# The first norm of a transformer block: single loads, VectorE normalization, grouped transposes, and a query part moved behind the first scores

## The chip, the cores and the metric

The kernel runs on one NeuronCore of a Trainium2 chip. The core's engines each have an instruction queue of their own that runs in order: TensorE (PE; its weight loads are listed apart as PEld), VectorE (DVE), ScalarE (ACT), GpSimd (POOL) and SyncE (SP, which here only issues DMA transfers). The metric is the device time of one execution in microseconds. Three runs of the kernel before gave 1083.71, 1084.04 and 1085.92 us; the median is 1084.04 us.

## What is computed

One block over x of shape (2, 1024, 256): a self-attention with 16 heads of 64, a cross-attention to a context of shape (2, 154, 192), and a gated feed-forward. All numbers are 32-bit floats. Only the beginning matters here:

```python
h = _layernorm(x, ln1_g, ln1_b)        # (x - mean) * rsqrt(var + eps) * g + b, over the 256 features
q, k, v = h @ sa_wq, h @ sa_wk, h @ sa_wv
attn = softmax(q @ k.T * 64 ** -0.5)   # per head
x = (attn @ v) @ sa_wo + sa_bo + x
```

## The kernel before

The rows of one batch are 8 tiles of 128 rows. A tile is taken with the one 4 places on: the order is 0, 4, 1, 5, 2, 6, 3, 7, so that a pair (i, 4+i) fills both halves of the partitions after its transposition.

**The first norm** (`norm_pieces`, with `first` set) has four pieces. `stats` (L239, L240) finds mean and variance of a tile on DVE. `deviation` (L245, L249) takes a pair: DVE adds eps, POOL raises to the power -0.5. `normalize` takes a pair: DVE makes an offset (L255), then ACT normalizes one tile (L269) and POOL the other (L266). `turn` transposes a pair on PE, 4 transposes into two PSUM banks (L279); its `store` then applies gain and shift while it copies to `hT`, half of it on DVE (L290), half on ACT (L294). Gain and shift are columns loaded by four small transfers (L109).

**The first unit.** A unit is one batch and one pair of heads; there are 16. Its queries and keys are projections of `hT`. For the very first unit, `part(what, i)` projects the columns of pair i (16 matmuls of 128 columns, L361) and `take` copies a finished bank to `q_sa` or `k_sa`. The kernel projects queries and keys of pairs 0 and 1, keys of pairs 2 and 3, and the rest of the queries later.

**The self-attention steps.** Steps p = 0 to 127, eight for each unit, are written out by hand. `self_first(p)` issues on PE the scores of the step in two banks (32 matmuls, L492; called s0, s1, ... below), and on DVE a maximum for each bank (L501). `then()` issues on ACT the exponentials (L507), which free the two score banks one after the other. SP exchanges the maxima and sums between partitions by four small transfers `st<-st` (L517); from the next step on POOL (L525, L526, L612), ACT (`ee`, L532) and DVE (L604, and the block transposes L639) finish the weights of earlier steps. There are only two score banks, so the second half of s(p+1) waits for the last exponential of step p.

Between the scores of two steps PE does other work. `run_work` takes it from a list, `work`, in order, one piece that needs two PSUM banks per step: the rest of the queries (`self_queries`), the values of the first unit in two pieces (`value_pieces`, L392), then the queries, the keys and the values of the next unit. The two banks (`mm`) are shared by all these pieces: a piece may start when ACT has copied the result of the one before. One piece of a second list, `side`, goes with it: the context transposes (`pc`, L201), context keys (`pk`, L776), `p_rows` (L192). From p = 7 on the step's other work is the weighted values `po` (L546).

Copies of finished pieces stand in `stores` and are issued by `flush(stores)`, in the next step ahead of the exponentials.

**SP's order.** SP issues `x`, the small columns, `sa_wq`, `sa_wk`, `sa_wv` (L133) and so on. Transfers take eight completion semaphores in turn, so the ninth transfer on SP and ACT together is issued only when the first has landed. At step 0 the keys' weights of the second unit are loaded behind the exchange of step 0, and at step 1 its queries' weights behind the exchange of step 1.

In the compiled program PE's order from the first scores on is: s0, rest of the queries, pc, s1, values (first half), pk, s2, values (second half), pk x2, s3, queries of unit 1, p_rows, s4, keys of unit 1, s5, values of unit 1, s6, pk x2, s7, pk, po.

Of the kernel before, what the change touches and what calls it, by code (L numbers as in the profile page):

```python
# [18 lines left out]
def tile_transformer_block(ctx: ExitStack, tc: tile.TileContext, a: dict, out: bass.AP):  # L19
# [59 lines left out]
        for b in range(B) for g in range(NG)  # L79
    }  # L80

    def load_x(queue, b, t):

        queue.dma_start(
            out=xt[b, t // GT][:, t % GT:t % GT + 2, :],
            in_=x[b, t * P:(t + 2) * P, :].rearrange("(t p) d -> p t d", p=P),
        )


# [11 lines left out]
            n_cols = r + k  # L101
        r += k
    rows = pp_.tile([n_rows - n_cols, P], F32, tag="P", name="rows")
    for t in range(0, NT // 2, 2):
        load_x(nc.sync, 0, t)
        load_x(nc.scalar, 0, NT // 2 + t)
    for n in names[:2]:
        for r0 in range(0, P, HR):
            (nc.scalar if n == names[0] else nc.sync).dma_start(  # L109
# [110 lines left out]
    def norm_pieces(kind, b, first=False):  # L220
# [30 lines left out]

        def normalize(t):
            rstd = st["rstd", t]
            off = small.tile([P, 2], F32, tag="off", name=f"off_{ln}_{b}_{t}")
            nc.vector.scalar_tensor_tensor(  # L255
                off, st["mv", t][:, :, 0], -1.0, rstd, op0=ALU.mult, op1=ALU.mult
            )
            pool, tag = (one, "xn") if narrow(kind, b) and not first else (pp_, "P")

            xn = pool.tile([P, nh, 2, D // nh], F32, tag=tag, name=f"xn_{ln}_{b}_{t}")  # L260
            st["xn", t] = xn
            for i in range(2):
                xs = xt[b, order[t + i] // GT][:, order[t + i] % GT, :]
                xs, own = xs.rearrange("p (c d) -> p c d", c=nh), xn[:, :, i, :]
                if not narrow(kind, b) or first and i == 1:
                    nc.gpsimd.tensor_scalar(  # L266
                        own, xs, rstd[:, i:i + 1], off[:, i:i + 1], op0=ALU.mult, op1=ALU.add)
                else:
                    nc.scalar.activation(  # L269
                        own, xs, AF.Identity, bias=off[:, i:i + 1], scale=rstd[:, i:i + 1])  # L270

        def turn(t):

            n = 2 if first else 1
            bank = mm_tile if first and t == 2 else spare["bank"]
            ph = [bank(f"ph_{ln}_{b}_{t}_{i}") for i in range(n)]
            for i in range(2 * D // P):

                nc.tensor.transpose(  # L279
                    ph[i * n * P // (2 * D)][:, i % (2 * D // P // n) * P:][:, :P],  # L280
                    st["xn", t].rearrange("p c i d -> p (c i d)")[:, i * P:(i + 1) * P], ident)

            def store():
                k = NC * 2 * P // nh
                for c in range(nh):
                    own = st["hT"][:, c, t // 2 * k:(t // 2 + 1) * k]
                    turned = ph[c * n // nh][:, c % (nh // n) * k:][:, :k]
                    gain, shift = cols[:, g0 + c:g0 + c + 1], cols[:, b0 + c:b0 + c + 1]
                    if spare["turned"] or first and c < nh // 2:
                        nc.vector.tensor_scalar(  # L290
                            own, turned, gain, shift, op0=ALU.mult, op1=ALU.add
                        )
                    else:
                        nc.scalar.activation(own, turned, AF.Identity, bias=shift, scale=gain)  # L294

            return store
# [12 lines left out]
    def narrow(kind, b):  # L309

        return kind == "sa" or kind == "ca" and b < B - 1
# [929 lines left out]
    with tc.manual_schedule():  # L1241
# [19 lines left out]
        def take(what, i):  # L1261
            at = banks[what] if i < 2 else banks["k2"]
            take_both(qk["sa", 0, 0]["qk".index(what)], at, scale if what == "q" else None,
                      i * P, 2 * P, shared=True)


        for _ in range(27):
            nc.tensor.transpose(own[0][:, 1, :P], ident, ident)
        emit(stats[0], stats[1], deviation[0])
        emit(stats[2], stats[3], normalize[0], deviation[1], stats[4], normalize[1])  # L1270
        copies = [turn[0](), turn[1]()]
        copies[0]()
        part("q", 0)
        part("k", 0)
        emit(stats[5], deviation[2])
        copies[1]()
        emit(stats[6], normalize[2], stats[7], deviation[3])
        copies = turn[2]()
        part("q", 1)
        emit(normalize[3])  # L1280
        copies()
        part("k", 1)
        copies = turn[3]()
        banks["k2"] = two_banks("first_k")
        part("k", 2)
        copies()
        take("q", 0)
        take("k", 0)
        part("k", 3)
# [7 lines left out]
        side.append((True, (), lambda: together(*(  # L1297
            lambda pr=pr: context_keys(pr, sum_tile) for pr in (1, 2)))))
        side.append((True, (), turn_rows))
        work.append(costing(2, lambda: self_queries(*units[0], P, 2 * P)))  # L1300
        work.extend(value_pieces(*units[0], 2, False))

        for p in range(SA):
# [5 lines left out]
            then = self_first(p)  # L1309
            flush(stores)  # L1310
            then()
            if adds:
                adds.pop(0)()
            flush(kept)
# [190 lines left out]
```

## Time and profile before

| | |
|---|---|
| median of three runs | 1084.04 us |
| profiled execution | 1085.11 us, span of its instructions 1083.3 us |
| PE busy | 1067.4 us, 99% of the span |
| DVE, ACT, POOL busy | 889.9, 646.9, 765.0 us |
| granted TensorE clock | 1.0 |

A row of the timeline gives the start in us from the beginning of the span, the duration, engine, line, operation, what is written and read, and how many instructions the row merges. In brackets stands how long the engine was idle before it, and what ended that. The view of waits sums such idle times: us in total, times, longest. Lines in these views are those of the kernel before.

### The profile page before, as it was taken

The numbers are of one execution on the slowest core, as the hardware profiler recorded it, in microseconds if no ns is written. First come the engines' busy times: TensorE is split into PE (matmuls) and PEld (weight loads), VectorE is DVE, ScalarE is ACT, GpSimd is POOL, SyncE is SP. The second block draws the span as 40 slices with busy tenths as digits, with TensorE's granted clock in tenths as the row PEclk, the third lists the DMA queues.
The fourth block names the chain that finished last, engine by engine and source line by source line (L and its number), as shares of the span: only waits on it lengthen the run. The fifth ranks groups of instructions, "written<-read, shape, count | busy, mean of one in ns | idle before, by whom it ended". The sixth has DMA issues, their size and how long they took to land.

```text
span 1083.3 us, 45246 instructions
## 1 busy us (share of the span) xinstructions
PE 1067.4 (99%) x18548; PEld 710.0 (66%) x18548; DVE 889.9 (82%) x1317; ACT 646.9 (60%) x2063; POOL 765.0 (71%) x1600
## 2 busy tenths in 40 slices
PE   8999999999999999999999999998999999999998
PEld 6556556566565565565675665575777767888998
DVE  5789999998998989999999989968877887655554
ACT  5666767677666666666776766666566554342221
POOL 2667777788777777777777777757665686388774
PEclk9999999999999999999999999999999999999999
DMA  3232111111111111211211201136855545000000
GB/s 94 64 90 62 44 43 44 37 38 43 33 43 24 43 43 33 48 42 29 48 41 26 53 14 37 24 96 139 202 134 138 126 115 131 17 6 15 20 11 30
DMA packets 105120, 62.84 MB, mean 58 GB/s; under 512 B 32266, under 2 KB 95506, under 8 KB 104914
## 3 DMA queue, kind: packets, MB, share of 16 engines
q1 hardware_dynamic: 103586, 59.29, 23.2%
q8 instruction: 146, 2.39, 0.9%
q10 hardware_dynamic: 1328, 0.66, 0.2%
q14 instruction: 60, 0.49, 0.1%
HBM read 30.01 MB, written 2.10 MB: 30 GB/s over the span
## 4 chain that ended last, share of the span: by engine, by line
PE 87%; DVE 3%; DMA 3%; POOL 3%; ACT 2%; SPq 1%; issue 1%; DVEq 0%; POOLq 0%; ACTq 0%
PE s L492 19%; PE po L546 19%; PE py_sa L466 5%; PE py_ca L466 5%; PE pv_sa L392 5%; PE pq_ca L361 4%; PE pq_sa L361 4%; PE pk_sa L361 4%; PE poc L938 4%; PE pb L1062 3%; PE pf L1186 3%; PE sc L855 3%; PE pa L1062 2%; PE pc L1062 2%; DMA st<-st 2%; PE pf L1225 1%
## 5 line engine op out<-in xcount | busy, mean ns | idle before, releaser
L612 POOL TENSOR_SCALAR p<-p,rd,ee 128x512 f32<-128x512 f32 x508 | 387.3, 773 | 99.1 <-DVE rd L604 97.3
L507 ACT ACTIVATE p<-s,st 128x512 f32<-128x512 f32 x512 | 345.8, 686 | 176.5 <-DVE st L501 170.5
L501 DVE TENSOR_REDUCE st<-s 128x2 f32<-128x1024 f32 x256 | 308.5, 1206 | 51.7 <-issue 20.1
L639 DVE STREAM_TRANSPOSE pT<-p 128x1024 f32<-128x1024 f32 x256 | 302.3, 1219 | 1.5 <-POOL p L612 1.5
L492 PE MATMUL s<-k_sa,q_sa 64*32 64x512 f32 x4096 | 255.4, 591 | 2.7 <-ACT p L507 2.1
L546 PE MATMUL po<-pT,v_sa 64*32 64x256 f32 x8192 | 238.6, 376 | 0.9 <-ACT p L873 0.9
L546 PEld LDWEIGHTS po<-pT,v_sa 64*32 64x32 f32 x8192 | 173.8, 106 | 74.9 <-issue 27.3
L492 PEld LDWEIGHTS s<-k_sa,q_sa 64*32 64x32 f32 x4096 | 81.6, 106 | 102.8 <-issue 53.5
L873 ACT ACTIVATE p<-sc,neg 128x154 f32<-128x154 f32 x256 | 96.5, 408 | 84.5 <-DVE rden L881 80.7
L884 POOL TENSOR_SCALAR p<-p,rden 128x154 f32<-128x154 f32 x256 | 97.3, 401 | 62.7 <-DVE rden L881 62.3
L507 ACT ACTIVATION_READ_ACCUMULATOR p<-s,st 128x1 f32 x512 | 103.2, 202 | 0.0
L525 POOL TENSOR_TENSOR dd<-st 128x8 f32<-128x8 f32 x128 | 25.8, 202 | 66.1 <-DMA st<-st 64.3
L392 PEld LDWEIGHTS pv_sa<-sa_wv,hT_ln 64*128 64x128 f32 x1024 | 58.6, 188 | 14.2 <-issue 10.9
L392 PE MATMUL pv_sa<-sa_wv,hT_ln 64*128 64x128 f32 x1024 | 61.8, 275 | 0.0
L860 DVE TENSOR_REDUCE neg<-sc 128x6 f32<-128x924 f32 (+1 forms) x48 | 48.0, 1001 | 14.5 <-PE sc L855 14.4
L466 PE MATMUL py_ca<-ca_wo,o_ca 128*128 128x256 f32 x256 | 59.9, 382 | 0.0
L466 PE MATMUL py_sa<-sa_wo,o_sa 128*128 128x256 f32 x256 | 59.5, 386 | 0.0
L466 PEld LDWEIGHTS py_sa<-sa_wo,o_sa 128*128 128x128 f32 x256 | 47.3, 190 | 17.8 <-issue 6.9
L361 PE MATMUL pq_ca<-hT_ln,ca_wq 64*128 64x512 f32 (+1 forms) x352 | 58.4, 590 | 0.5 <-DMA ca_wq<-in_L_xattn_ca_wq_dram 0.5
L873 ACT ACTIVATION_READ_ACCUMULATOR p<-sc,neg 128x1 f32 x256 | 57.2, 224 | 0.0
L361 PE MATMUL pq_sa<-hT_ln,sa_wq 64*32 64x512 f32 (+1 forms) x976 | 57.0, 586 | 0.0
L361 PE MATMUL pk_sa<-hT_ln,sa_wk 64*32 64x512 f32 x960 | 56.8, 590 | 0.0
(135 smaller groups left out, 1471.5 us busy)
## 6 DMA issues: line engine op xcount, KB each, us to landing
wf<-pT_ca SPq DMA_DIRECT2D x128, 128.0 KB, 2.4
v_sa<-v_sa SPq DMA_DIRECT2D x32, 256.0 KB, 3.8
st<-st SPq DMA_DIRECT2D x510, 1.0 KB, 1.9
sa_wq<-in_L_xattn_sa_wq_dram SPq DMA_DIRECT2D x32, 128.0 KB, 3.4
sa_wk<-in_L_xattn_sa_wk_dram SPq DMA_DIRECT2D x32, 128.0 KB, 3.6
sa_wv<-in_L_xattn_sa_wv_dram SPq DMA_DIRECT2D x32, 128.0 KB, 3.3
ca_wq<-in_L_xattn_ca_wq_dram SPq DMA_DIRECT2D x32, 128.0 KB, 4.4
wf<-in_L_xattn_ff_w_dram SPq DMA_DIRECT2D x12, 256.0 KB, 4.2
```

The lines of the kernel that those rows point to most:

```text
L361: nc.tensor.matmul(pq[r][f:f + m, at:at + n], lhsT=wt[own, c, f:f + m], rhs=h[own, c, t0:t0 + n], start=(c == 0), stop=(c == NH - 1), tile ...
L392: nc.tensor.matmul(pv[r][:, i * P:(i + 1) * P], lhsT=h[own, c, i * P:(i + 1) * P], rhs=wt[own, c, :], start=(c == 0), stop=(c == NH - 1), ...
L466: nc.tensor.matmul(py[:, e * D:(e + 1) * D], lhsT=o[:, i, (t + e) * P:(t + e + 1) * P], rhs=wo[kind, b, g][:, i, :], start=(i == 0), stop= ...
L492: nc.tensor.matmul(sc[a4 * KB:(a4 + 1) * KB, j, :], lhsT=q[r, c:c + KB], rhs=k[r, h * HB:(h + 1) * HB], start=True, stop=True, tile_positi ...
L501: nc.vector.tensor_reduce(st[:, 0, 0, i, :], sc, AX.X, ALU.max, negate=True)
L507: nc.scalar.activation(pr[:, j, :], sc[:, j, :], AF.Exp, bias=st[:, 0, 0, i, j:j + 1], accum_out=st[:, 0, 1, i, j:j + 1],)
L546: nc.tensor.matmul(po[a2][d:d + KB, :QH // 2], lhsT=v[r, t, e, d:d + KB], rhs=pT[r, d // DH * NK + n, :], start=(t == 0 and e == 0), stop= ...
L612: nc.gpsimd.tensor_scalar(pr[:, j, :], pr[:, j, :], v["rd"][:, c:c + 1], v["ee"][:, 0, c:c + 1], op0=ALU.mult, op1=ALU.mult,)
L639: nc.vector.transpose(halves[h][:, :, c:c + KB], slot[p]["members"][i].rearrange("p j (n k) -> p (j n) k", k=KB))
L873: nc.scalar.activation(pr_[:, j, i, :T], sc[:, j, i * T:(i + 1) * T], AF.Exp, bias=neg[:, j, i:i + 1], accum_out=den[:, j, i:i + 1],)
L884: nc.gpsimd.tensor_scalar(pr_[:, j, i, :T], pr_[:, j, i, :T], rden[:, j, i:i + 1], 1.0, op0=ALU.mult, op1=ALU.mult,)
L1062: nc.tensor.matmul(into[:, :BT], lhsT=lhs, rhs=wh[pair][i], start=first, stop=True, skip_group_check=True)
```

## The change

1. The first loads: each of SP and ACT loads one tile, one tile and two tiles, instead of two and two. That is six transfers instead of four ahead of the columns and the weights.
2. `normalize` of the first norm runs on DVE alone, two instructions per pair that subtract the mean and multiply by the reciprocal deviation. The offset, the ACT and the POOL instruction fall away.
3. The pieces are issued in another order. On DVE: statistics of tiles 0, 4, 1 and 2, the normalization of pair 0, statistics of 5 and 6, the copy of pair 0, statistics of 3 and 7, the normalization of pairs 1, 2 and 3, their copies. On PE: transposes of pair 0, keys 0, queries 0, transposes of pairs 1, 2 and 3 in a row, keys 1, 2 and 3. Pairs 2 and 3 take one bank each. The filling transposes ahead are 23 instead of 27.
4. Queries of pair 1 are no longer projected before the first scores. The later piece covers 384 columns per half instead of 256. It is issued in step 0 directly, behind the exponentials, with its copy flushed at once, and is no longer an entry of `work`; so step 0 also takes the first entry that is left.

In the compiled program PE's order from the first scores on becomes: s0, rest of the queries (384), values (first half), pc, s1, values (second half), pk, s2, queries of unit 1, pk x2, s3, keys of unit 1, p_rows, s4, values of unit 1, s5, s6, pk x2, s7, pk, po. From there on the order is the same. SP still loads the queries' weights of unit 1 behind the exchange of step 1; the moves of the value tiles (L408, L409) come one step earlier in its queue. ACT's first activation is now the copy of pair 0, and its table load waits for the four column transfers; before it waited for the first x.

```diff
-    def load_x(queue, b, t):
+    def load_x(queue, b, t, n):
         queue.dma_start(
-            out=xt[b, t // GT][:, t % GT:t % GT + 2, :],
-            in_=x[b, t * P:(t + 2) * P, :].rearrange("(t p) d -> p t d", p=P),
+            out=xt[b, t // GT][:, t % GT:t % GT + n, :],
+            in_=x[b, t * P:(t + n) * P, :].rearrange("(t p) d -> p t d", p=P),
         )
...
-    for t in range(0, NT // 2, 2):
-        load_x(nc.sync, 0, t)
-        load_x(nc.scalar, 0, NT // 2 + t)
+    for t, n in ((0, 1), (1, 1), (2, 2)):
+        load_x(nc.sync, 0, t, n)
+        load_x(nc.scalar, 0, NT // 2 + t, n)
...
         def normalize(t):
             rstd = st["rstd", t]
+            if first:
+                xn = st["xn", t] = pp_.tile(
+                    [P, nh, 2, D // nh], F32, tag="P", name=f"xn_{ln}_{b}_{t}")
+                for i in range(2):
+                    xs = xt[b, order[t + i] // GT][:, order[t + i] % GT, :]
+                    nc.vector.tensor_scalar(
+                        xn[:, :, i, :], xs.rearrange("p (c d) -> p c d", c=nh),
+                        st["mv", t][:, i, 0:1], rstd[:, i:i + 1],
+                        op0=ALU.subtract, op1=ALU.mult)
+                return
...
         def turn(t):
-            n = 2 if first else 1
+            n = 2 if first and t < GT else 1
...
         def take(what, i):
             at = banks[what] if i < 2 else banks["k2"]
             take_both(qk["sa", 0, 0]["qk".index(what)], at, scale if what == "q" else None,
-                      i * P, 2 * P, shared=True)
-        for _ in range(27):
+                      i * P, P if what == "q" else 2 * P, shared=True)
+        for _ in range(23):
             nc.tensor.transpose(own[0][:, 1, :P], ident, ident)
-        emit(stats[0], stats[1], deviation[0])
-        emit(stats[2], stats[3], normalize[0], deviation[1], stats[4], normalize[1])
-        copies = [turn[0](), turn[1]()]
+        emit(stats[0], stats[1], deviation[0], stats[2], stats[4], normalize[0])
+        emit(stats[3], stats[5], deviation[1])
+        copies = turn[0]()
+        copies()
+        part("k", 0)
+        part("q", 0)
+        emit(stats[6], deviation[2], stats[7], deviation[3])
+        emit(normalize[1], normalize[2], normalize[3])
+        copies = [turn[1](), turn[2]()]
         copies[0]()
-        part("q", 0)
-        part("k", 0)
-        emit(stats[5], deviation[2])
         copies[1]()
-        emit(stats[6], normalize[2], stats[7], deviation[3])
-        copies = turn[2]()
-        part("q", 1)
-        emit(normalize[3])
+        copies = turn[3]()
+        part("k", 1)
         copies()
-        part("k", 1)
-        copies = turn[3]()
         banks["k2"] = two_banks("first_k")
         part("k", 2)
-        copies()
         take("q", 0)
         take("k", 0)
         part("k", 3)
...
-        work.append(costing(2, lambda: self_queries(*units[0], P, 2 * P)))
         work.extend(value_pieces(*units[0], 2, False))
...
             then = self_first(p)
             flush(stores)
             then()
+            if p == 0:
+                run(lambda: self_queries(*units[0], P, P))
+                flush(stores)
```

More of the change, by code (lines that the diff above doesn't have):

```diff
@@ L257, in normalize @@
             )
-            pool, tag = (one, "xn") if narrow(kind, b) and not first else (pp_, "P")
+            pool, tag = (one, "xn") if narrow(kind, b) else (pp_, "P")
             xn = pool.tile([P, nh, 2, D // nh], F32, tag=tag, name=f"xn_{ln}_{b}_{t}")
@@ L264, in normalize @@
                 xs, own = xs.rearrange("p (c d) -> p c d", c=nh), xn[:, :, i, :]
-                if not narrow(kind, b) or first and i == 1:
+                if not narrow(kind, b):
                     nc.gpsimd.tensor_scalar(
```

## The prediction

> **What bounds the kernel now.** I read the page's busy times first, then the waits of PE over the whole span, then PE's timeline through the first steps, and last the other queues at the places where PE's next piece would have to wait.
>
> ```profile
> PE 1067.4 (99%) x18548; PEld 710.0 (66%) x18548; DVE 889.9 (82%) x1317; ACT 646.9 (60%) x2063; POOL 765.0 (71%) x1600
> ```
>
> ```profile
> PE s L492 <- ACT p L507: 2.1, 5, 1.1
> PE ph_ln L279 <- POOL xn_ln L266: 2.0, 5, 0.9
> PE first L1268 <- POOL ident masks.py:199: 1.9, 1, 1.9
> ...
> PE s L492 <- DVE k_sa L382: 0.6, 1, 0.6
> ```
>
> PE is busy for 99% of the span, so only its idle time, or work taken from it, can be won, and any new idle time is lost. The second fence is PE's longest waits over the whole span. Most of the 2.0 and all of the 0.6 lie ahead of the first scores; they are what an earlier first norm can take away. The longest of the 2.1, 1.1, is the first place where the softmax, not PE, sets the pace.
>
> ```profile
> 9.48 1.16 PE L361 MATMUL first<-hT_ln,sa_wq 64*128 64x128 f32 x16
> 10.48 1.06 PE L361 MATMUL first<-hT_ln,sa_wk 64*128 64x128 f32 x16
> ...
> 14.24 0.66 PE L279 MATMUL ph_ln<-ident,xn_ln 128*128 128x128 f32 x4
> 14.82 2.06 PE L361 MATMUL first_k<-hT_ln,sa_wk 64*128 64x128 f32 x32
> 17.52 1.95 PE L492 MATMUL s<-k_sa,q_sa 64*32 64x512 f32 x32 [0.64 <-DVE k_sa L382]
> 19.40 2.00 PE L361 MATMUL pq_sa<-hT_ln,sa_wq 64*128 64x256 f32 x16
> 21.33 0.74 PE L201 MATMUL pc<-ident,cn 77*96 77x77 f32 x8
> 22.00 1.96 PE L492 MATMUL s<-k_sa,q_sa 64*32 64x512 f32 x32
> 23.89 2.06 PE L392 MATMUL pv_sa<-sa_wv,hT_ln 64*128 64x128 f32 x32
> 25.88 1.34 PE L776 MATMUL pk<-ctxT,ca_wk 96*128 96x320 f32 x4
> ...
> 31.11 2.42 PE L776 MATMUL pk<-ctxT,ca_wk 96*128 96x320 f32 x8
> 33.46 1.95 PE L492 MATMUL s<-k_sa,q_sa 64*32 64x512 f32 x32
> 35.20 3.64 PE L361 MATMUL pq_sa<-hT_ln,sa_wq 64*32 64x512 f32 x64
> ```
>
> Read these starts as a budget, each piece from its own start to the next: a projection of one pair 1.0 us, four transposes 0.6, the scores of a step 1.9, the rest of the queries 1.9, pc 0.7, half the values 2.0, pk 1.3, two pk 2.35, a projection of 64 matmuls 3.45 (3.64 with its overlap). From 17.52 on no row has a bracket: each piece's inputs were there in time. That is the state which the new order must not lose.
>
> **The change, part by part.** I call the start of the first scores T: 17.52 before. I walk PE's new order to the first weighted values (po), since from there the orders agree.
>
> *The start.* These are SP's and ACT's rows, and two of DVE.
>
> ```profile
> 4.46 1.26 SPq L133 DMA_DIRECT2D sa_wq<-in_L_xattn_sa_wq_dram  x2
> 6.03 1.25 SPq L133 DMA_DIRECT2D sa_wk<-in_L_xattn_sa_wk_dram  x2
> ```
>
> ```profile
> 4.13 0.43 DVE L239 BATCH_NORM_STATS2 st_ln<-x 128x6 f32<-128x256 f32 x1 [4.13 <-DMA x<-in_x_dram]
> ...
> 8.20 0.73 DVE L290 TENSOR_SCALAR hT_ln<-ph_ln,cols 128x128 f32<-128x128 f32 x2
> ...
> 15.36 0.41 DVE L373 TENSOR_SCALAR q_sa<-first 128x256 f32<-128x256 f32 x1
> ```
>
> ```profile
> 4.18 1.28 ACT L269 ACT_TABLE_LOAD   x1 [4.18 <-DMA x<-in_x_dram]
> ```
>
> With half as many bytes the first tile may land before 4.13; how much earlier, no row tells, but little of it can arrive at PE. DVE must pass the statistics of tile 2 before it normalizes pair 0, and tile 2 is in the last of the three loads, with as many bytes ahead of it as before. Two normalizations of 128x256 on DVE cost some 0.4 us each (nearest row: 15.36, 0.41). So I give the first transposes no gain, and the copy of pair 0, which stands behind two more statistics (0.43 each and small ones) on DVE, starts at about 8.4 against 8.20.
>
> Then PE wants keys 0, so it waits for `sa_wk`. Its two halves were issued at 6.03 and 6.65, because SP waited for x to land; all of x is no earlier, and two more transfers stand ahead, so I leave 6.65. No row gives its landing; it is below 10.48, where PE used it without a wait, and above 6.65 plus 2.9 (the same kind of load, quoted below), 9.55. I take 9.75, nearer to the quoted one. ACT's table load, 1.28 us, now begins only when the columns are there (no later than 8.20), so ACT's half is ready at 9.9 at the latest, when keys 0 need it in their second half. From 9.75: keys 0 and queries 0 2.0, three transposes 1.75, keys 1 to 3 3.0, and the copy 0.64 as before, T = 17.15. Change: -0.4 us. Bounds: 16.2 (-1.3) if the copy of pair 0 at 8.8 sets it, 17.9 (+0.4) if `sa_wk` lands at 10.48. The eight DVE normalizations (8 x 0.4) replace ACT and POOL work; those of pairs 1 to 3 lie beside keys 0 and queries 0. From 8.4: the copy 0.75, two statistics with their small ones 1.4, six normalizations at most 2.4, so the last ends at 12.95, when PE reaches the transposes of pair 3 (9.75 + 2.0 + 1.2 = 12.95): just covered, and each 0.1 more on DVE would move T by 0.1. The four filling transposes are nothing: PE waits behind them either way.
>
> *The later queries.* 16 matmuls of 384 instead of 256 columns: 1.93 x 1.5 = 2.9, so +0.95. The 1.0 that queries of pair 1 cost earlier is already taken out of T.
>
> *Values behind the queries.* Both pieces use the same two banks. ACT can copy the queries out only behind the exponentials of step 0.
>
> ```profile
> 22.70 0.67 ACT L376 ACTIVATE q_sa<-pq_sa 128x256 f32<-128x256 f32 x2
> ...
> 26.52 0.69 ACT L507 ACTIVATE p<-s,st 128x512 f32<-128x512 f32 x1
> 27.09 0.21 ACT L507 ACTIVATION_READ_ACCUMULATOR p<-s,st 128x1 f32 x1
> ```
>
> The copies begin 5.18 us behind T (22.70 - 17.52) and take about 0.95 for 2 x 384 columns, so the values start at T + 6.15. PE is through with the queries at T + 1.9 + 2.9 = T + 4.8. Wait: 1.35 us. Before, pc and s1 stood between, so the values never waited here. Bounds 0.7 (first bank alone) to 1.6.
>
> Values (2.0) and pc (0.7) now precede s1, which starts at T + 8.8 instead of T + 4.48. That alone costs PE nothing, but everything hanging on s1 is 4.3 us later: its exponentials (22.00 to 27.2, 5.2 us behind s1's start) end at T + 14.0, and SP's exchange of step 1 waits for them.
>
> *The queries' weights of unit 1.* They are the next in SP's queue.
>
> ```profile
> 27.97 2.47 SPq L517 DMA_DIRECT2D st<-st  x4
> 30.48 1.34 SPq L133 DMA_DIRECT2D sa_wq<-in_L_xattn_sa_wq_dram  x2
> ```
>
> ```profile
> DMA to landing us min/median/max: 2.9/2.9/2.9
> ```
>
> The last line is `sa_wq` between 28 and 40 us. The exchange takes 2.5 (27.97 to 30.48), the second half is issued 0.65 later and lands in 2.9: T + 14.05 + 2.5 + 0.65 + 2.9 = T + 20.1. PE's order is s1 (T + 8.8 to 10.7), values 12.7, pk 13.95, s2 15.85, and then at once these queries. Before, they landed at 30.48 + 0.65 + 2.9 = 34.0, and PE came to them at 35.20, having done one more step. So the cover of 1.2 us becomes a wait of 4.25 us. Queued behind it in PE: two pk, s3 and with it the whole softmax; nothing passes. Bounds: 2.5 (if a half lands 1 us earlier and the exchange issues at once) to 5.2.
>
> The Trainium skill ("DMA: Bandwidth & Descriptors", "Anatomy of one DMA — SWDGE (gpsimd) path") gives 2.0 us plus bytes / 436 GB/s for a transfer of the other queue kind; for 128 KB that is an estimate of 2.3 against the 2.9 of the row. By it this wait is 3.65 and the sum below 7.3; I keep the row.
>
> *An empty step.* The list `work` is used up one step sooner, and between s5 and s6 nothing is left.
>
> ```profile
> 23.20 2.36 DVE L501 TENSOR_REDUCE st<-s 128x2 f32<-128x1024 f32 x2 [2.13 <-PE s L492]
> ...
> 36.99 2.36 DVE L639 STREAM_TRANSPOSE pT<-p 128x1024 f32<-128x1024 f32 x2
> ```
>
> ```profile
> 46.23 3.84 PE L392 MATMUL pv_sa<-sa_wv,hT_ln 64*128 64x128 f32 x64
> 50.00 1.95 PE L492 MATMUL s<-k_sa,q_sa 64*32 64x512 f32 x32
> 51.87 2.42 PE L776 MATMUL pk<-ctxT,ca_wk 96*128 96x320 f32 x8
> 54.26 1.09 PE L492 MATMUL s<-k_sa,q_sa 64*32 64x512 f32 x16
> 56.46 1.09 PE L492 MATMUL s<-k_sa,q_sa 64*32 64x512 f32 x16 [1.11 <-ACT p L507]
> 57.49 1.34 PE L776 MATMUL pk<-ctxT,ca_wk 96*128 96x320 f32 x4
> 58.76 3.68 PE L546 MATMUL po<-pT,v_sa 64*32 64x256 f32 x128
> ```
>
> From s5's start to the release of its first bank: 1.2 to the maximum (22.00 to 23.20), 1.3 to the first exponential, two exponentials of 0.67, 3.85 in all; s5 itself takes 1.9. So PE waits 1.95 ahead of s6, and another 0.4 ahead of its second half (two more exponentials, 1.35, against 0.95 of matmuls): 2.35. Before, 3.8 us of values lay there (46.23 to 50.00). Bounds 1.7 to 3. One step on, s7's wait of 1.11 becomes about 0.5, since PE now comes later to it: behind s6, DVE does its two transposes (2.36) and the maxima, and two pk (2.35) cover most. That is -0.6; bounds -1.1 to +0.5.
>
> **Sum:** -0.4 + 0.95 + 1.35 + 4.25 + 2.35 - 0.6 = +7.9 us at po, with no idle time behind it that could take it back: the other four waits for exponentials are 2.1 - 1.1 = 1.0 us together. The profiled execution, 1085.11 (span 1083.3), becomes 1093.0. It lies 1.07 above the median, so for the median 1084.04 + 7.9 = 1091.9.
>
> **The rivals.**
> - *Faster: the start runs dense.* If `sa_wk` were there by 7.7, PE would go without a gap through four transposes (2.4), five projections (5.0) and the copy (0.64) from some 7.1 (9.48 less two transposes and the copies): T = 15.1, -2.4 us; with the s7 wait gone and the weights of unit 1 early, -2.4 + 0.95 - 1.1 = -2.55, 1081.5. It decides only if those weights land before T + 15.85, that is, are issued 4.3 us sooner. SP's order, the exchange ahead of them, speaks against it. Chance 0.04.
> - *No change.* The same with T from the walk and the new waits covered: -0.4 + 0.95 - 0.6, about 1084. Against it stand three waits, of which each needs another accident to vanish. Chance 0.05.
> - *Slower, but the weights arrive in time.* Without the 4.25: +3.65, 1087.7. It needs the exponentials of step 1 four us sooner. Chance 0.13.
> - *Slower still: the clock falls in the new wait.* No wait of PE before is longer than 1.9 us, so the trace does not show what a gap of 4.25 does to its clock. Were PE at half speed for some 3.4 us of work behind a gap of 4.25, +1.7: 1093.6. The Trainium skill ("TensorE: Matmul & The Clock Gate", "What you observe" and what follows) states that rule: half clock after an idle window of about 3.4 us, which runs freely, so a gap of 4.25 need not hold a whole one. No run here shows it so far. Chance 0.15.
>
> **How the numbers follow.** My forecast has 0.63. A measurement of this kernel tells about 0.2% (2.2 us) from no change. Slower holds 0.63 + 0.13 + 0.15 = 0.91, less a little for all bounds low together, 0.89; same 0.06; faster 0.05. The terms at their low ends give -1.3 + 0.95 + 0.7 + 2.5 + 1.7 - 1.1 = +3.45, at their high ends +11.6; both at once are unlikely. The range reaches from the third rival, 1087.0, to 1094.5, which holds the fourth.
>
> **What would show it.** Right: s0 at about 17.1; a wait of PE of over 1 us ahead of the first values; a wait of about 4 us ahead of the queries of unit 1, ended by the load of `sa_wq`, with SP's load behind the exchange of step 1; s5 and s6 in a row with PE idle for 2 us between; po at about 66.4 instead of 58.76. Wrong: `sa_wq` landed before s2 ends; s0 before 16; or PE idle in some later place that was covered before.

## The result and the profile after

The changed kernel takes 1096.68 us (median of 4 runs, 1095.75 to 1097.9), the kernel before 1084.03 us beside it; the ratio is 1.0112 with a 95% interval of 1.0096 to 1.0128. It is slower, by 12.6 us, where 7.9 had been forecast, and lies above the forecast's range. Its profiled execution took 1096.72 us, with a span of 1094.9, 11.6 more than before.

PE's timeline of the changed kernel up to the first weighted values. Lines are ten higher than before: L502 is the scores, L371 a projection, L402 the values, L556 `po`, and L1278 the filling transposes (L1268 before).

```profile
1.91 4.91 PE L1278 MATMUL first<-ident 128*128 128x128 f32 x23 [1.91 <-POOL ident masks.py:199]
7.85 0.66 PE L289 MATMUL ph_ln<-ident,xn_ln 128*128 128x128 f32 x4 [1.04 <-DVE xn_ln L259]
9.57 2.53 PE L371 MATMUL first<-hT_ln,sa_wk 64*128 64x128 f32 x15 [1.06 <-DMA sa_wk<-in_L_xattn_sa_wk_dram]
11.91 1.80 PE L371 MATMUL first<-hT_ln,sa_wq 64*128 64x128 f32 x15
13.64 1.53 PE L289 MATMUL ph_ln<-ident,xn_ln 128*128 128x128 f32 x12
...
18.69 1.95 PE L502 MATMUL s<-k_sa,q_sa 64*32 64x512 f32 x32 [0.64 <-DVE k_sa L392]
20.57 2.85 PE L371 MATMUL pq_sa<-hT_ln,sa_wq 64*128 64x384 f32 x16
24.36 2.43 PE L402 MATMUL pv_sa<-sa_wv,hT_ln 64*128 64x128 f32 x32 [0.93 <-ACT q_sa L386]
...
27.38 1.95 PE L502 MATMUL s<-k_sa,q_sa 64*32 64x512 f32 x32
...
32.52 1.95 PE L502 MATMUL s<-k_sa,q_sa 64*32 64x512 f32 x32
38.08 6.95 PE L371 MATMUL pq_sa<-hT_ln,sa_wq 64*32 64x512 f32 x64 [3.61 <-DMA sa_wq<-in_L_xattn_sa_wq_dram]
44.95 2.42 PE L786 MATMUL pk<-ctxT,ca_wk 96*128 96x320 f32 x8
...
62.52 1.09 PE L502 MATMUL s<-k_sa,q_sa 64*32 64x512 f32 x16 [2.06 <-ACT p L517]
63.86 1.09 PE L502 MATMUL s<-k_sa,q_sa 64*32 64x512 f32 x16 [0.24 <-ACT p L517]
...
70.74 3.68 PE L556 MATMUL po<-pT,v_sa 64*32 64x256 f32 x128
```

All three new waits stand where the prediction put them: 0.93 ahead of the values, 3.61 ahead of the queries of unit 1, 2.06 and 0.24 at s6. s7, at 67.23, no longer waits. But two pieces of work are longer than they ever were before: keys 0 and queries 0 take from 9.57 to 13.64, 4.07 us instead of 2.0, and the queries of unit 1 from 38.08 to 44.95, 6.87 instead of the 3.57 of before (35.20 to 38.77; the prediction reckoned with 3.45). Much of the reason is in the view of windows (start and end, length, busy us of PE, PEld, DVE, ACT and POOL with their instructions, PE's granted clock, then the DMA's share and GB/s), cut close to where the clock changes:

```profile
6.57:9.98 3.41, 1.31 (x9) 0.72 (x7) 3.30 (x12) 2.09 (x3) 0.70 (x1) 0.98 0.67 173
9.98:13.39 3.41, 3.26 (x30) 3.15 (x30) 2.84 (x11) 0.00 (x0) 1.62 (x2) 0.52 0.29 81
33.70:37.11 3.41, 0.77 (x16) 0.00 (x0) 2.77 (x4) 2.13 (x7) 1.81 (x4) 1.00 0.12 28
37.11:40.52 3.41, 2.44 (x17) 0.67 (x25) 0.89 (x1) 0.75 (x3) 1.99 (x5) 0.50 0.22 58
40.52:43.93 3.41, 3.41 (x40) 0.98 (x32) 0.00 (x0) 0.00 (x0) 0.00 (x0) 0.50 0.47 86
```

The clock was halved twice, for about 3.4 us behind the gaps of the norm and for about 6.8 us behind the wait for the weights; in finer windows the falls begin at 9.83 and 37.14. In the profile of before it is 1.0 in both stretches. The same stretch over the norm, and PE's rows in it, are there

```profile
6.57:9.98 3.41, 1.94 (x19) 1.36 (x19) 2.59 (x13) 2.28 (x6) 2.00 (x4) 1.00 0.74 204
```

```profile
1.91 4.92 PE L1268 MATMUL first<-ident 128*128 128x128 f32 x27 [1.91 <-POOL ident masks.py:199]
7.40 0.63 PE L279 MATMUL ph_ln<-ident,xn_ln 128*128 128x128 f32 x4 [0.57 <-POOL xn_ln L266]
8.93 0.63 PE L279 MATMUL ph_ln<-ident,xn_ln 128*128 128x128 f32 x4 [0.90 <-POOL xn_ln L266]
```

PE is busy for 1.94 instead of 1.31, and no stretch of 3.41 us between 4 and 15 us has less than 1.9. The difference is not that of 27 fills and 23: the filling ends at 6.83 and at 6.82. It takes 0.21 us for each transpose at first and 0.11 later, and the faster part begins at about 5.7 us in the execution of before and at about 6.4 in the other (the view of windows shows a clock of 1.00 all the while). The difference lies behind the filling: before, PE does eight transposes in this stretch and starts queries 0 at 9.48; now it does four and starts keys 0 at 9.57.

At `po` the changed kernel is 70.74 - 58.76 = 12.0 us behind. The pieces, each as the difference between its row and the row of before: start of the first scores +1.17; later queries +0.95; wait ahead of the values 0.93, and 0.35 by which the values themselves run longer (2.35 instead of 2.0); wait for the weights +3.61; those queries, 6.87 for 3.57, +3.30; s6 +2.30; s7 -1.11. That is 11.5; the remaining 0.5 is spread over other pieces. Behind `po` nothing more is lost: the spans differ by 11.6.

What became of the first tile's earlier landing, and why the weights of unit 1 came late, is in DVE's and SP's rows:

```profile
3.40 0.43 DVE L239 BATCH_NORM_STATS2 st_ln<-x 128x6 f32<-128x256 f32 x1 [3.40 <-DMA x<-in_x_dram]
...
6.53 0.43 DVE L239 BATCH_NORM_STATS2 st_ln<-x 128x6 f32<-128x256 f32 x1 [1.21 <-DMA x<-in_x_dram]
6.99 0.18 DVE L240 BATCH_NORM_AGGREGATE mv_ln<-st_ln 128x2 f32<-128x6 f32 x1
7.09 0.70 DVE L259 TENSOR_SCALAR xn_ln<-x,mv_ln,rstd_ln 128x256 f32<-128x256 f32 x2
```

```profile
6.68 1.26 SPq L133 DMA_DIRECT2D sa_wk<-in_L_xattn_sa_wk_dram  x2
...
32.65 2.47 SPq L527 DMA_DIRECT2D st<-st  x4
35.16 1.34 SPq L133 DMA_DIRECT2D sa_wq<-in_L_xattn_sa_wq_dram  x2
```

The first tile is there at 3.40 instead of 4.13, but the statistics of tile 2 stand ahead of the first normalization and wait until 6.53 for the last load; the first transposes start at 7.85, before at 7.40. The second unit's `sa_wq` is issued behind the exchange of step 1, at 35.16 instead of 30.48.

### The profile page after: what moved, and what is told of

Read it like the earlier page. It is cut to its first block, busy times and chain, and to the rows that moved or that the text cites. A ratio compares the mean times of both kernels' runs of the same rounds, so it can differ in the third digit from the quotient of the medians.

```text
span 1094.9 us, 45195 instructions
## 1 busy us (share of the span) xinstructions
PE 1072.7 (98%) x18528; PEld 708.3 (65%) x18528; DVE 890.6 (81%) x1321; ACT 643.9 (59%) x2059; POOL 759.6 (69%) x1596
## 4 chain that ended last, share of the span: by engine, by line
PE 81%; DVE 4%; ACT 4%; DMA 4%; POOL 3%; SPq 2%; issue 1%; ACTq 0%; DVEq 0%; POOLq 0%
PE s L502 16%; PE po L556 16%; PE py_sa L476 5%; PE py_ca L476 5%; PE pv_sa L402 5%; PE pq_sa L371 4%; PE poc L948 4%; PE pk_sa L371 4%; PE pq_ca L371 4%; PE pb L1072 3%; PE pf L1196 3%; DMA st<-st 3%; PE sc L865 3%; ACT p L517 3%; PE pa L1072 2%; PE pc L1072 2%
## 5 line engine op out<-in xcount | busy, mean ns | idle before, releaser
L502 PE MATMUL s<-k_sa,q_sa 64*32 64x512 f32 x4096 | 253.9, 591 | 4.2 <-ACT p L517 3.4
L556 PE MATMUL po<-pT,v_sa 64*32 64x256 f32 x8192 | 237.7, 376 | 1.3 <-ACT p L883 1.3
L556 PEld LDWEIGHTS po<-pT,v_sa 64*32 64x32 f32 x8192 | 174.6, 106 | 74.4 <-issue 29.5
L502 PEld LDWEIGHTS s<-k_sa,q_sa 64*32 64x32 f32 x4096 | 79.4, 106 | 106.2 <-issue 57.6
L402 PEld LDWEIGHTS pv_sa<-sa_wv,hT_ln 64*128 64x128 f32 x1024 | 58.8, 188 | 15.0 <-issue 11.7
L371 PE MATMUL pq_sa<-hT_ln,sa_wq 64*32 64x512 f32 (+1 forms) x976 | 61.1, 611 | 3.6 <-DMA sa_wq<-in_L_xattn_sa_wq_dram 3.6
L402 PE MATMUL pv_sa<-sa_wv,hT_ln 64*128 64x128 f32 x1024 | 62.1, 275 | 0.9 <-ACT q_sa L386 0.9
L371 PE MATMUL pq_ca<-hT_ln,ca_wq 64*128 64x512 f32 (+1 forms) x352 | 58.2, 589 | 0.0
L371 PE MATMUL pk_sa<-hT_ln,sa_wk 64*32 64x512 f32 x960 | 56.3, 590 | 0.4 <-ACT q_sa L386 0.3
```

Source lines behind the costliest of these rows:

```text
L371: nc.tensor.matmul(pq[r][f:f + m, at:at + n], lhsT=wt[own, c, f:f + m], rhs=h[own, c, t0:t0 + n], start=(c == 0), stop=(c == NH - 1), tile ...
L402: nc.tensor.matmul(pv[r][:, i * P:(i + 1) * P], lhsT=h[own, c, i * P:(i + 1) * P], rhs=wt[own, c, :], start=(c == 0), stop=(c == NH - 1), ...
L502: nc.tensor.matmul(sc[a4 * KB:(a4 + 1) * KB, j, :], lhsT=q[r, c:c + KB], rhs=k[r, h * HB:(h + 1) * HB], start=True, stop=True, tile_positi ...
L556: nc.tensor.matmul(po[a2][d:d + KB, :QH // 2], lhsT=v[r, t, e, d:d + KB], rhs=pT[r, d // DH * NK + n, :], start=(t == 0 and e == 0), stop= ...
```

## The experiments

Twelve kernels ran. The theory: the slowdown is the prediction's three waits plus two falls of the clock, and the clock falls because PE is idle for too much of some 3.4 us, not because of the new instructions. The rivals were that the weights' lateness has another cause than the exchange of step 1, that the slow queries are slow because of traffic or shape, and that the norm itself costs or wins more than the clock. Ratios are to the kernel before, in brackets their 95% intervals; T is the start of the first scores in the profiled execution.

**One entry in the list.** An empty piece ahead of the values puts every later piece back one step, where the weights were loaded for it.

```diff
+        work.append(costing(2, lambda: None))
         work.extend(value_pieces(*units[0], 2, False))
```

> The changed kernel with an empty entry at the head of the list of work, so that step 0 issues the later queries and the context transposes only and each later piece stays in the step where it was before the change. Theory (the cost lies in the pieces that moved one step forward): no wait ahead of the first values (0.9 us and 0.35 more within them), none for the queries' weights of unit 1 (3.6), these queries at full clock (3.4 less), s6 covered again (2.3 less), and the wait of 1.1 at s7 back; 1096.7 - 11.6 + 1.1 + 0.3 = about 1086.5. Rival (the norm and the late start of the scores are the main cost): at most 3 us less, 1094 or more.

Measured: 1087.79 us, 1.0033 [1.0016, 1.0051]. All three waits are gone:

```profile
19.00 1.95 PE L502 MATMUL s<-k_sa,q_sa 64*32 64x512 f32 x32 [0.64 <-DVE k_sa L392]
20.89 2.85 PE L371 MATMUL pq_sa<-hT_ln,sa_wq 64*128 64x384 f32 x16
24.66 1.95 PE L502 MATMUL s<-k_sa,q_sa 64*32 64x512 f32 x32 [0.26 <-ACT q_sa L386]
...
37.76 3.64 PE L371 MATMUL pq_sa<-hT_ln,sa_wq 64*32 64x512 f32 x64
```

The queries of unit 1 start without a bracket and take 3.64, as before the change. So 8.9 of the 12.6 us (1096.68 - 1087.79) hang on the step in which the pieces stand. T is still late, 19.00, with the clock at 0.50 from 10.9 to 14.3.

**The wait filled with work.** 24 transposes of the identity stand ahead of the queries of unit 1, in a bank of their own.

```diff
+            if p == 2:
+                fill = sum_tile("fill")
+                for _ in range(24):
+                    nc.tensor.transpose(fill[:, :P], ident, ident)
```

> The changed kernel with 24 filling transposes on PE (about 3.5 us at the 0.145 us of one in the first norm) ahead of the queries of unit 1, where PE sits idle for 3.6 us waiting for their weights. Theory (the clock is halved because PE is idle): the wait stays, the granted clock stays 1.0 and the 64 matmuls take 3.45 instead of 6.9 us; 1096.7 - 3.4 = 1093.3. Rival (these matmuls are slow because of something else, the transfers that run beside them): they stay at 6.9 us and the time is 1096.7 or a little more.

Measured: 1093.75 us, 1.0083 [1.0068, 1.0098].

```profile
36.02 2.84 PE L1334 MATMUL fill<-ident 128*128 128x128 f32 x24
39.68 4.48 PE L371 MATMUL pq_sa<-hT_ln,sa_wq 64*32 64x512 f32 x64 [0.82 <-DMA sa_wq<-in_L_xattn_sa_wq_dram]
```

The weights are as late as they were, and the transposes produce nothing, yet 2.9 us come back: the clock is 1.00 from 38 to 46, and the queries take 4.4 instead of 6.9. The queries start 19.4 behind T in both kernels (39.68 - 20.31, 38.08 - 18.69). Traffic and shape were unchanged, so they are not what lowers the clock here; PE's idle time is. The next piece starts at 44.09: at full clock these queries still take 4.4, not 3.57, since they start on the first half of the weights and the second half comes later. So of the 3.30 some 2.5 (6.87 - 4.41) are the clock and 0.8 belongs to the wait for the weights. In this execution the first fall, in the norm, lasted two windows, and T was 20.31, so the profile shows less than the whole gain.

**The other weights first.** The second unit's `sa_wq` is loaded at step 0 and its `sa_wk` at step 1.

```diff
-        ahead[0] = lambda: load_weights("sa", units[1][1], "k")
-        ahead[1] = lambda: load_weights("sa", units[1][1], "q")
+        ahead[0] = lambda: load_weights("sa", units[1][1], "q")
+        ahead[1] = lambda: load_weights("sa", units[1][1], "k")
```

> The changed kernel with the two loads of unit 1 exchanged: queries' weights at step 0, keys' weights at step 1. Theory: the queries' weights land 7 us before PE needs them, so the wait of 3.6 us goes and with it the half clock, 3.4 us: 1096.7 - 7.0 = 1089.7; the keys' weights are not missed, since a step lies between. Rival (PE would wait there anyway, for a bank or for the softmax): a wait of similar length with another releaser, 1094 or more.

Measured: 1090.58 us, 1.0054 [1.0039, 1.0069], 6.1 below the changed kernel.

```profile
24.46 2.43 PE L402 MATMUL pv_sa<-sa_wv,hT_ln 64*128 64x128 f32 x32 [0.93 <-ACT q_sa L386]
...
34.37 3.64 PE L371 MATMUL pq_sa<-hT_ln,sa_wq 64*32 64x512 f32 x64
...
55.51 1.09 PE L502 MATMUL s<-k_sa,q_sa 64*32 64x512 f32 x16 [2.06 <-ACT p L517]
```

The wait for the weights and its slow queries are gone, 3.61 + 3.30 = 6.9 by the profiles; the waits at the values and at s6 are what they were. So the lateness came from SP's order: issued one exchange sooner, the load is waited for no more.

**The norm's gaps filled.** 30 filling transposes ahead instead of 23, and eight behind the transposes of pair 0.

```diff
-        for _ in range(23):
+        for _ in range(30):
...
         copies = turn[0]()
+        for _ in range(8):
+            nc.tensor.transpose(own[0][:, 1, :P], ident, ident)
         copies()
```

> The changed kernel with 30 instead of 23 filling transposes ahead and 8 more behind the transposes of pair 0, so that PE is hardly idle between 1.9 us and keys 0. Theory (the two gaps of 1.04 and 1.06 us halve the clock from about 9.9 to 13.9 us): keys 0 and queries 0 take 2.0 instead of 4.1 us, the first scores start at about 16.6 instead of 18.7, the time is 1096.7 - 2.0 = 1094.7. Rival (the half clock there is the late warm-up of the chip, whatever PE does, or DVE sets the start): first scores no earlier than 18, 1096 or more.

Measured: 1095.93 us, 1.0104 [1.0089, 1.0119]. The clock stayed at 1.00 through the norm and T was 17.35, 1.35 earlier:

```profile
9.84 1.52 PE L371 MATMUL first<-hT_ln,sa_wk 64*128 64x128 f32 x15 [0.36 <-DVE hT_ln L300]
...
12.30 1.53 PE L289 MATMUL ph_ln<-ident,xn_ln 128*128 128x128 f32 x12
```

Keys 0 and queries 0 take 2.46 at full clock, so 1.6 of the 4.07 in the changed kernel are the clock. But the time fell by 0.75 only, a miss against 2. The profiled execution, at 1095.41 one of the two lower of four, is 1.3 us below that of the changed kernel, as much as T moved; in rows further on two differences all but cancel:

```profile
36.70 6.01 PE L371 MATMUL pq_sa<-hT_ln,sa_wq 64*32 64x512 f32 x64 [3.58 <-DMA sa_wq<-in_L_xattn_sa_wq_dram]
...
60.21 3.30 PE L502 MATMUL s<-k_sa,q_sa 64*32 64x512 f32 x32 [2.06 <-ACT p L517]
```

The queries of unit 1 take 5.95 up to the next piece instead of 6.87, since this fall lasted one window only. s6 behind its wait takes 3.23 instead of 2.36, and the two pk behind it 2.83 instead of 2.35: the clock fell there, from 61.0 to 64.4, where it had not fallen in the changed kernel's profile.

**Parts 1 to 3 alone**, with the queries of pair 1 projected early and the list as before.

```diff
-                      i * P, P if what == "q" else 2 * P, shared=True)
+                      i * P, 2 * P, shared=True)
...
+        part("q", 1)
         part("k", 1)
...
+        work.append(costing(2, lambda: self_queries(*units[0], P, 2 * P)))
...
-            if p == 0:
-                run(lambda: self_queries(*units[0], P, P))
-                flush(stores)
```

> The first three parts of the change alone: single loads, VectorE normalization, transposes of pairs 1 to 3 in a row; queries of pair 1 are projected ahead of keys 1 again, and the later queries are the first entry of the list of work, as before the change. Theory (the norm costs what the start of the first scores shows, the moved query part the rest): first scores at 18.7 + 1.0 = 19.7 against 17.5, nothing else changes, 1084.6 + 2.2 = 1086.8, with the clock halved between about 10 and 14 us as in the changed kernel. Rival (the new norm order is what upsets the steps behind it): waits ahead of the values or of the queries of unit 1 also here, 1090 or more.

Measured: 1088.55 us, 1.0029 [1.0018, 1.0040], between the two expectations. No new waits behind T, but T = 20.06, 2.5 behind the kernel before: the clock fell to half at 10.5.

**Part 4 alone**, on the kernel before.

```diff
-                      i * P, 2 * P, shared=True)
+                      i * P, P if what == "q" else 2 * P, shared=True)
...
-        part("q", 1)
...
-        work.append(costing(2, lambda: self_queries(*units[0], P, 2 * P)))
...
             then()
+            if p == 0:
+                run(lambda: self_queries(*units[0], P, P))
+                flush(stores)
```

> The fourth part of the change alone, on the kernel before: the later query part of 384 columns issued in step 0, no projection of queries of pair 1 ahead of the first scores. Theory: first scores 1.0 us earlier, the later queries 0.9 longer, 1.3 for the values, 3.6 for the weights, 3.4 for the halved clock behind that wait, 2.3 between s5 and s6, less 1.1 at s7: +9.4 us, 1094.0; with the clock dropping only in part down to 1091. Rival (the part is harmless without the late norm): within 2 us of before.

Measured: 1098.16 us, 1.0114 [1.0099, 1.0129], as slow as the whole change and 4 us above what was expected of it; T was 17.54, not the 16.5 that the expectation counts with.

```profile
37.03 6.89 PE L361 MATMUL pq_sa<-hT_ln,sa_wq 64*32 64x512 f32 x64 [3.65 <-DMA sa_wq<-in_L_xattn_sa_wq_dram]
...
61.82 1.09 PE L492 MATMUL s<-k_sa,q_sa 64*32 64x512 f32 x16 [2.46 <-ACT p L507]
63.16 1.96 PE L492 MATMUL s<-k_sa,q_sa 64*32 64x512 f32 x16 [0.25 <-ACT p L507]
```

With the norm as before, all three waits and the slow queries are there, so the move of the queries is the costly part. The two parts do not add up (3.5 and 13.1 us against 12.6). In the profile of part 4 alone the clock falls a second time behind s6's wait (s6's second half 1.96 instead of 1.09), in the changed kernel's it does not, and falls in the norm instead.

**Both repairs**, the list entry and the 30 + 8 fills; and then the first loads in pairs again.

```diff
-    for t, n in ((0, 1), (1, 1), (2, 2)):
+    for t, n in ((0, 2), (2, 2)):
```

> The changed kernel with the empty entry in the list of work and with the 30 and 8 filling transposes, so without moved pieces and without a halved clock in the norm. Theory (what is left of the change is a start that gains nothing): first scores at 17.35 as with the filling alone, the later queries 0.9 longer, a wait of 0.3 ahead of s1: 1087.8 - 1.65 = 1086.1, 0.5 to 2 us over the kernel before. Rival (the change is a gain once its two accidents are taken away): 1083 or less.

> The same with the first loads in pairs again (two and two tiles). Theory (single loads only bring the first tile earlier; the last tile and, behind it in SP's order, the keys' weights come 0.6 us later, and these set keys 0): DVE starts at 4.1 instead of 3.4, but keys 0 start some 0.6 us earlier, first scores at about 16.8, 1085.5. Rival (the earlier first tile is a real gain): first scores at 17.9 or later, 1086.7.

Measured: 1086.94 us, 1.0019 [1.0010, 1.0029], and with loads in pairs 1086.61 us, 1.0011 [1.0000, 1.0022]. The clock is 1.00 throughout in both profiles, T is 17.14 and 17.23. Loads in pairs let DVE start at 4.50 instead of 3.35, and still it reaches the first normalization at 6.87, against 6.88: single first loads win nothing. The expected 0.6 us did not come.

**One gap filled at a time**: 30 fills ahead and none behind (first), or 23 ahead and eight behind (second). The second is

```diff
         copies = turn[0]()
+        for _ in range(8):
+            nc.tensor.transpose(own[0][:, 1, :P], ident, ident)
         copies()
```

and the first the other half of the fills shown above.

> The changed kernel with 30 filling transposes ahead instead of 23, so that PE is busy up to the first transposes and only the wait of about 1.06 us for sa_wk is left. Theory: it was the two waits of 1.04 and 1.06 us together, 2.1 idle out of 2.7 us, that halved the clock; one of them alone does not. Then the granted clock stays at 1.0 from 8 to 16 us, keys 0 and queries 0 take 2.0 to 2.5 us, the first scores start by 17.3 and the time is about 1095.5. Rival: any single wait of a microsecond does it. Then keys 0 and queries 0 take 3.5 us or more, the first scores start at 18.2 or later and the time is 1096.5 or more.

> The changed kernel with eight filling transposes between the transposes of pair 0 and keys 0, so that the wait of 1.06 us for sa_wk is all but filled, and the wait of 1.04 us for the normalization ahead of them stays. Theory (both waits together are needed): the clock stays at 1.0 from 8 to 16 us, the first scores start by 17.3, time about 1095.5. Rival (one wait is enough, or the window had begun before): the clock falls to 0.5 somewhere between 8 and 14 us and the first scores start at 18 or later, 1096.5 or more.

Measured: 1096.12 us, 1.0104 [1.0087, 1.0121], and 1096.06 us, 1.0104 [1.0089, 1.0119]; T = 17.18 and 17.27 and the clock 1.00 up to 16 in both. So in the changed kernel the norm's fall took both gaps together, 2.1 idle of 2.7 us; with either one filled it did not come in these executions (the last run shows that it can). The times fell by 0.6 only; the windows of the first kernel show a part of the reason (the first line is the norm, the last two s6):

```profile
7.05:10.46 3.41, 2.06 (x18) 1.62 (x18) 3.27 (x14) 2.09 (x3) 0.99 (x2) 1.00 0.67 192
34.35:37.76 3.41, 1.04 (x13) 0.49 (x21) 1.53 (x2) 2.01 (x7) 3.17 (x8) 1.00 0.29 80
37.76:41.17 3.41, 3.41 (x44) 1.95 (x36) 0.00 (x0) 0.00 (x0) 0.00 (x0) 0.50 0.14 25
58.24:61.65 3.41, 1.25 (x24) 0.35 (x32) 3.41 (x5) 2.88 (x9) 2.75 (x6) 1.00 0.44 78
61.65:65.06 3.41, 3.41 (x19) 1.20 (x8) 3.25 (x5) 1.81 (x5) 2.59 (x5) 0.50 0.35 80
```

The fall at s6 costs 1.65 here (s6 and two pk take 6.36 from 60.15 on instead of 4.71), more than the 1.5 won at T. The two falls here begin at 37.76 and 61.65, 23.9 us apart, seven times 3.41. In the changed kernel they begin at 9.83 and 37.14, 27.3 apart, eight times 3.41. In the second kernel's profile the clock falls a third time at 724.06, behind a wait of 1.99 us for exponentials of the cross-attention; that is 662.18 us, 194 times 3.413, behind its fall at 61.88. The windows thus run on a beat of their own, and which of the kernel's gaps fills most of a window is a matter of its phase.

**Queries 0 ahead of keys 0**, with the fills, the list entry and the loads in pairs.

```diff
-        part("k", 0)
         part("q", 0)
+        part("k", 0)
```

> The changed kernel with the list of pieces shifted back by one step (an empty first entry), the fills of 30 and 8, the first loads in pairs, and queries 0 projected ahead of keys 0, since sa_wq is issued 1.7 us ahead of sa_wk. Theory: the projections then start when the copy of pair 0 is there, at about 9.4, with no wait for a load, the first scores start at about 16.9, and the time is 0.3 us below the kernel with keys first: about 1086.3, level with the kernel before within 0.2%. Rival: the order before the first scores still holds a gain over the kernel before once every wait is filled, first scores by 16.0 and 1083 or less.

Measured: 1087.0 us, 1.0014 [1.0004, 1.0023]. T = 16.93, and PE runs from 7.60 to the copy ahead of the first scores without a bracket. That is 0.6 earlier than before, and `po` starts at 58.88 against 58.76: the longer later queries (+0.95) and s1's wait of 0.27 take it back, less what s7 waits shorter (0.34 for 1.11). The order has no gain left to release; that the span ends 2.0 us later, behind `po`, is not explained by any one wait. (Ahead of a later `po`, at 712 to 714 us, PE waits 1.2 to 1.8 us for exponentials in the three repaired kernels and 0.9 before, which is a part of it.)

**Four fills.** The prediction had costed the four filling transposes that the change takes away at nothing. Here they are back, in the kernel with parts 1 to 3 alone.

```diff
-        for _ in range(23):
+        for _ in range(27):
```

> The changed kernel with the queries projected as in the kernel before (as in the run with the norm's parts alone), and with 27 filling transposes ahead as before instead of 23. The text on record cost the four at nothing, since PE waits behind them either way. Theory of the clock: PE's busy time is summed over windows of about 3.41 us, and a window less than about half busy is followed by half clock. With four fills more, the window from the last fills to keys 0 is about 2.05 of 3.41 busy instead of 1.15 to 1.7, whatever its phase. Then the granted clock stays at 1.0 from 8 to 16 us, keys 0 and queries 0 take 2.0 to 2.5 us instead of 4.1, the first scores start at 18.2 to 18.5 instead of 20.06, and the time is about 1086.8, 1.7 below the run with 23. Rival: four fills ahead of a wait are nothing, the clock falls as it did, first scores at 19.5 or later, and the time is 1088.5.

Measured: 1086.78 us, 1.0018 [1.0005, 1.0030]. The median came as expected, but by chance: it is the middle between 1086.14 and 1087.42, and no execution lies there. The profiled execution did not come as expected: in it T was 19.49 and the clock fell, at 10.56, behind 3.41 us of which PE was busy for 2.16; the windows shown lie 0.34 us ahead of the fall, and the one that ends at it has the same 2.16.

```profile
6.81:10.22 3.41, 2.16 (x16) 1.52 (x16) 3.31 (x14) 2.09 (x3) 0.79 (x2) 1.00 0.68 187
10.22:13.63 3.41, 3.41 (x32) 3.19 (x31) 2.44 (x9) 0.00 (x0) 1.53 (x2) 0.55 0.32 87
```

The single executions tell it better. Of the 12 with four more fills, six had a mean clock of 1.0 and took 1085.06 to 1086.14 us, six had 0.996 to 0.998 and took 1087.42 to 1090.34. With 23 fills one of 10 had 1.0 (1085.92), nine had 0.995 to 0.998, from 1086.02 to 1091.8. The kernel before kept 0.999 or 1.0 in all 42 executions beside these two; of the 13 beside three other kernels one had 0.998. That four transposes which only fill a wait shift how often the clock falls is suggested by these counts, not shown: they are few, and the mean over the span does not say where the clock fell. What they do show is that 27 fills in the new order do not keep the clock as 27 in the old order did. The middles of the two groups lie 3.6 us apart, more than the 1.6 of one window; by estimate one window at half clock lowers the mean by 0.0016 (half of 3.41 of some 1086 us), so 0.996 and 0.997 stand for two or more.

## Why the prediction was wrong

The direction, to which the prediction gave 0.89, was right, and the three waits came where and because it said. The size was not: 7.9 us forecast, 12.6 measured. At `po` the difference is 12.0 - 7.9 = 4.1, and the two falls of the clock, 1.6 and 2.5, are 4.1; that they fill it so exactly is luck, since the errors of the other terms (+0.2 at the weights, -0.5 at s7, 0.5 spread over other pieces) cancel.

- **The step that failed: the sum costs all of PE's work at full clock**, the projections behind the new wait and those of the norm too. What the prediction says of the clock is its fourth rival, "the clock falls in the new wait", held apart from the sum at a price of 1.7 us and a chance of 0.15. The fall came, and it cost 2.5 us, because the clock stayed at half for two windows, and the second held nothing but work. The wait filled with transposes shows the cause: the weights as late, the clock at 1.0, 2.9 us less.
- **The clock also fell where no rival stood**, in the norm, at a cost of 1.6. The walk takes keys 0 and queries 0 at 2.0, as before, though its new order leaves PE idle for 2.1 of the 2.7 us ahead of them; with either gap filled, or both, the clock held in six profiles and fell in one, the last run's. Why this fall had no rival: the text looked for a gap longer than any before, and these were two of 1.04 and 1.06 us, little longer than the 0.90 in a row of before. "The four filling transposes are nothing: PE waits behind them either way" leaves out that idle time can cost more than its length, but how much these four are worth is open: with them, half of the executions of the norm alone kept the full clock, without them one in ten.
- **The Trainium skill** ("TensorE: Matmul & The Clock Gate", "What's actually happening") says that the clock halves after an idle window of about 3.4 us, that windows are 3413 ns and run freely, and that it returns after a busy one. The length and the free beat agree with the falls here (23.9, 27.3 and 662.18 us apart, about 3.4 or 6.8 long). That the window must be idle does not: it fell behind windows in which PE was busy for 0.45 to 2.16 of 3.41 us, and stayed low behind one of 2.44.
- **T**: -0.4 forecast (17.15), +1.17 measured (18.69). But for the clock the walk came out right, in part because the transfer covers a miss: pair 0's copy on DVE came at 8.91, not 8.4, but PE waited for `sa_wk`, and keys 0 started at 9.57 for 9.75. Where the gaps were filled and the clock held, T was 17.14 to 17.35. That the single loads win nothing, since tile 2 comes last, was right too.
- **Later queries**: +0.95, as forecast (20.57, 2.85).
- **Values behind the queries**: 1.35 forecast; 0.93 of wait and 0.35 in a slower first piece.
- **The weights of unit 1**: 4.25 forecast, for both halves; 3.61 measured to the first half and about 0.8 more within the queries. The mechanism and the place were right.
- **The empty step**: 2.35 forecast, 2.06 + 0.24 = 2.30 measured. s7: -0.6 forecast, -1.11 measured.
- The other rivals fell: no dense start, no cover for the waits, and the weights did not arrive in time.

What stays open: what exactly the clock goes by. Ten of the profiles have falls. Followed on its beat, the clock fell in them behind all 15 windows at full clock in which the records show PE busy for 0.45 to 1.67 of 3.41 us, and behind none with 1.68 or more, but for the one of 2.16 in the last run. (The first windows of a span, ahead of the first recorded change, and its end are left out.) So busy time separates the cases at about half a window, and one case shows that it is not the whole measure. Open too are the 1 to 2 us that the repaired kernels lose behind `po`. No version that ran is faster than the kernel before.

## What to carry to other kernels

Before a piece is moved one step ahead, look up in the other queues when its inputs are issued: here the transfer stood behind an exchange that had moved back 4.7 us (27.97 to 32.65), and one empty entry in a list was worth 8.9 us. Price every gap in PE by its length and by what follows it at half clock, and add up neighbouring gaps: two waits of a microsecond with little work between count as one. Work that only fills a wait can hold the clock: the 24 transposes won 2.9 us.

## What the runs showed of the hardware

The granted clock went from 1.0 to 0.5 on a beat of about 3.41 us, for one window or two, and cost about 1.6 us in one window full of projections and 2.5 in two, the first of which began idle. It fell behind windows in which PE was busy for up to 1.67 of 3.41 us, and once behind one of 2.16; filling transposes of the identity, 0.1 to 0.2 us each, put into a gap, held it there in seven profiles of eight. In six profiles the falls in the norm begin between 9.33 and 10.94 us, so the beat's phase differs between executions. That this is why a kernel with gaps near the border has two groups of times, here 1085.1 to 1086.1 and 1087.4 to 1090.3 us, is argued and not shown. With the norm's gaps filled, the clock fell at s6 instead in three profiles.
